# Layer 1's neighbour mix as one 512-column product, in a four-layer graph network on one Trainium2 core

## The chip, the core and the metric

The kernel runs on one core of one Trainium2 chip, in a single launch. The metric is device time in microseconds (us). Before the change three runs gave 3241.18, 3243.03 and 3243.22 us; the median is 3243.03 us. The profiled execution took 3241.16 us, with a span of 3239.2 us from the first to the last instruction and a mean granted TensorE clock of 0.999.

The engines have short names in profiles: PE is TensorE's matmul, PEld its weight load, DVE is VectorE, ACT is ScalarE, POOL is GpSimd, SP is the engine from whose queue nearly all transfers are issued.

## The reference

There are 128 independent batches of 128 nodes with 512 features each, all in float32, and one 128 x 128 adjacency matrix. Four layers follow each other, each with its input added and a layer norm over the features:

```python
x = layernorm(x + einsum('nm,bmd->bnd', adj, x) @ W0 + bias0)          # layer 0
x = layernorm(x + gat(x))                                              # layer 1
x = layernorm(x + maxpool(x))                                          # layer 2
x = layernorm(x + attention(x))                                        # layer 3

def gat(x):                       # W: 512 x 512, a: 1024
    h = x @ W1
    s1, s2 = h @ a[:512], h @ a[512:]
    e = leaky_relu(s1[:, :, None] + s2[:, None, :], 0.2) * adj
    att = softmax(e, axis=2)
    return elu(einsum('bij,bjf->bif', att, h) + beta * h)
```

Layer 2 takes, for every node, the largest value of adj @ x over the features, with a bias and a relu. Layer 3 is attention with 8 heads of 64, masked by adj, with one more layer norm inside it.

The kernel never computes h. In layer 1 it writes (att + beta * I) @ x @ W1: first a mix of the nodes of x, then one product with W1. The logits come from x @ (W1 @ a), two row sums per batch. Layer 0 is the same: a mix with adj, then a product with W0.

## The kernel before

Every batch is a chain of steps written as a Python generator. `use(engine, work, take)` asks a planner for a place in an engine's order and for buffers; the planner keeps estimated durations and fixes the order of all engines' instructions when the program is built. On the chip that order is fixed, and semaphores do the waiting. `LANDED` is the planner's allowance for the landing of turned features.

```python
FIRST, PAIRS = 2, 6            # groups of two batches at the start and at the end, else groups of four
SOON = (0, 4, 0, 4, 10, 0)     # how far the last groups' steps are brought forward
SCALED = 2                     # near the end, last layer norms are applied on ScalarE
BUFS = {"ps": 8, "x": 19, "yT": 4, "z": 2, "e": 2, "et": 1, "eT": 2, "ex": 2, "xT": 2, "v": 7,
        "qkT": 2, "pt": 1, "xt": 2}
LAST, AHEAD = 14, 4            # the last 14 batches get a rank 4 earlier
DIRECT = 12                    # layer 0 of the first 12 batches is mixed in the first way
LANDED = 4.0
```

A product needs the features on the partitions (yT, four blocks of 128). There are two ways to get there. The first gives it at once, with four products of 128 columns, in which x itself is the stationary operand; ScalarE copies the result out of PSUM:

```python
def mixed(xb, nodes, first=False):
    b0, b1 = yield use("PE", 0.9, lambda: ("ps", "yT"), late=0.2)
    p = bank(b0, K, P)
    for k in range(K):
        nc.tensor.matmul(p[:, k, :], xb[:, k * P : (k + 1) * P], nodes, start=True, stop=True)
    yT = buf(b1, K, P)
    # ... (first batch: copied in two halves)
    yield use("ACT", 0.6, urgent=True)
    nc.scalar.copy(yT, p)
    give(b0)
    return yT, b1
```

The second multiplies once, 512 columns wide, with the nodes' weights as the stationary operand. The result has nodes on the partitions, and has to be turned: VectorE transposes it in 32 x 32 blocks, one transfer writes it to DRAM, and four transfers read it back so that the blocks land on their partitions. The features then stand in a permuted order, and the weight's rows are loaded in the same order (`permuted`):

```python
def mixed_rows(xb, nodes):
    b0 = yield use("PE", 0.86, "ps", late=0.2)
    p = bank(b0, D)
    nc.tensor.matmul(p, nodes, xb, start=True, stop=True)
    bt = yield use("DVE", 0.71, "xt", urgent=True)
    xt = buf(bt, Q, P)
    nc.vector.transpose(xt.rearrange("p q f -> p (q f)"), p)
    give(b0)
    scratch = yield from to_squares(xt, bt)          # one transfer, 256 KB
    b1 = yield use("SP", 2.0, "yT", late=LANDED)
    yT = buf(b1, K, P)
    from_squares(yT, scratch)                        # four transfers, 64 KB each
    return yT, b1
```

The part of a batch that the change touches:

```python
    direct = i < DIRECT                                                     # layer 0
    yT, by = yield from mixed(xb, adjT, i == 0) if direct else mixed_rows(xb, adjT)
    # ... product with W0, bias, layer norm
    yield wa_ready                                                          # layer 1
    yield use("DVE", 1.7)
    for j in range(2):
        scr = one.tile([P, D], F32, name="scr")
        nc.vector.scalar_tensor_tensor(scr, xb, 1.0, wa_rows[:, j, :], ..., accum_out=gr.s[:, b, j : j + 1])
    done(gr.logits[h])

    yield gr.attention[h]
    yT, by = yield from mixed(xb, gr.eT[h][:, b % 2])
    gr.read(h, 2)
    bp = yield use("PE", 3.44, "ps", late=0.2)
    p = product(bp, lambda k: yT[:, k, :], lambda k: w1_sb[:, k, :])
    give(by)
    # ... elu, layer norm, layer 2
    # layer 3: x turned as in mixed_rows into xT; queries and keys for a whole group (128, 256 or
    # 512 columns), values, scores, softmax, turned weights, weighted values, projection, two norms
```

In `product` every matmul has 512 columns, and four of them add up over the features. Queries and keys (L621) are computed for a group at once: 512 columns in a group of four, 256 in a group of two. Each matmul of the source appears as two MATMUL instructions in the trace. Line numbers of the profile: L270 is `mixed`, L289 is `mixed_rows`, L292 its transpose, L281 ScalarE's copy in `mixed`, L262 `product`, L670 scores, L691 weighted values, L325 the writes to DRAM, L311 the four reads.

Of the kernel before, what the change touches and what calls it, by code (L numbers as in the profile page):

```python
# [8 lines left out]
F32 = mybir.dt.float32  # L9
# [6 lines left out]
P = 128  # L16
D = 512
K = D // P
G = 4
FIRST, PAIRS = 2, 6  # L20
SOON = (0, 4, 0, 4, 10, 0)
WHOLE = 2
SCALED = 2
H = 8
HD = D // H
S = 32
Q = P // S
# [4 lines left out]

BUFS = {
    "ps": 8,
    "x": 19, "yT": 4, "z": 2, "e": 2, "et": 1, "eT": 2, "ex": 2, "xT": 2, "v": 7, "qkT": 2,
    "pt": 1, "xt": 2,
}
LAST, AHEAD = 14, 4
DIRECT = 12
LATER = 18  # L40
LANDED = 4.0
MARGIN = 1.0
LAND, ROW_LAND = 2.0, 0.0053

# [6 lines left out]
class Plan:  # L51
# [14 lines left out]
    def use(self, engine, work, take=None, late=0.05, urgent=False, follow=False):  # L66

        names = take if callable(take) else lambda: (take,) if take else ()
        return engine, work, names, late, 0 if follow else 1 if urgent else 2
# [67 lines left out]
def gnn_stack_kernel(  # L141
# [17 lines left out]
    nc = tc.nc  # L159
# [3 lines left out]
    const = ctx.enter_context(tc.tile_pool(name="const", bufs=1))  # L163
    work = ctx.enter_context(tc.tile_pool(name="work", bufs=1))
    small = ctx.enter_context(tc.tile_pool(name="small", bufs=12))
    one = ctx.enter_context(tc.tile_pool(name="one", bufs=1))
    ps = ctx.enter_context(tc.tile_pool(name="ps", bufs=1, space=PSUM))

    plan = Plan()
# [2 lines left out]
    def buf(slot, *shape):  # L172
        return work.tile([P, *shape], F32, name="{}_{}".format(*slot))
# [153 lines left out]
    def from_rows(dst, scratch):  # L327

        nc.sync.dma_start(dst, scratch.rearrange("(a r) c f -> (r c) a f", a=Q))
# [47 lines left out]
    def matrix(dst, src):  # L377
        nc.sync.dma_start(dst, src.rearrange("(k p) o -> p k o", p=P))

    def loads():  # L380
        yield use("SP", 0.4)
        nc.sync.dma_start(adj_sb, adj)
        landing(adj_in, P // 4)
        yield from load(0, "ACT", nc.scalar)
        w0_slot.append((yield use("SP", 0.0, "qkT")))
        w0_nat.append(
            buf(w0_slot[0], G, 2 * K, P).rearrange("p b c n -> p (b c n)")[:, : K * D].rearrange(
                "p (k o) -> p k o", k=K
            )
        )  # L390
        for k in range(K):
            yield use("SP", 0.4)
            nc.sync.dma_start(w0_nat[0][:, k, :], w0[k * P : (k + 1) * P])
            landing(w0_chunk[k], P)
        yield from load(1)
        yield use("SP", 0.4)
        nc.sync.dma_start(bias0_sb, rows(bias0, D))
        landing(bias0_in, P)
        for i in range(2, 4):
            yield from load(i)  # L400
        slot = yield use("SP", 1.0, "pt")
        matrix(w1_sb, w1)
        a_sb = buf(slot, H, P).rearrange("p (s k) f -> p s (k f)", s=2)
        nc.sync.dma_start(a_sb, rows(a, 2 * D).rearrange("p (s f) -> p s f", s=2))
        landing(w1_in, (K + 2) * P)
        plan.start(logit_rows(a_sb, slot), 0)
        for i in range(4, 8):
            yield from load(i)
        yield use("SP", 2.0)
        permuted(w0_sb, w0)  # L410
        landing(w0_in, K * P)
        yield use("SP", 1.0)
        nc.sync.dma_start(beta1_sb, rows(beta1, 1))
        nc.sync.dma_start(
            b2_sb, bass.AP(tensor=b2.tensor, offset=b2.offset, ap=[[1, P], [1, 1]])
        )
        landing(scalars_in, 2 * P)
        for i in range(8, 12):
            yield from load(i)
        yield use("SP", 2.5)  # L420
        permuted(wqkv_sb, w_qkv)
        matrix(wproj_sb, w_proj)
        for dst, src in ((bproj_sb, b_proj), (gamma_sb, gamma), (beta3_sb, beta3)):
            nc.sync.dma_start(dst, rows(src, D))
        landing(w3_in, (4 * K + 3) * P)
        for i in range(12, NB):
            yield from load(i)
# [34 lines left out]
    def logit_rows(a_sb, slot):  # L462

        yield w1_in
        wa = const.tile([P, K, 2], F32, name="wa")
        for s in range(2):
            for k in range(K):
                yield use("DVE", 0.8)
                scr = one.tile([P, D], F32, name="scr")
                nc.vector.scalar_tensor_tensor(  # L470
                    scr, w1_sb[:, k, :], 1.0, a_sb[:, s, :], op0=ALU.mult, op1=ALU.mult,
                    accum_out=wa[:, k, s : s + 1],
                )
        give(slot)
        for s in range(2):
            b0 = yield use("PE", 0.5, "ps", late=0.2, urgent=True)
            p = bank(b0, K, P)
            for k in range(K):
                nc.tensor.transpose(p[:, k, :], wa[:, k, s : s + 1].to_broadcast([P, P]), ident)
            yield use("DVE", 0.7, urgent=True)  # L480
            nc.vector.tensor_copy(wa_rows[:, s, :], p.rearrange("p k f -> p (k f)"))
            give(b0)
        done(wa_ready)

# [58 lines left out]
    def attention1(gr, h):  # L543
        yield gr.logits[h]
        yield scalars_in
        s = gr.s

        yield use("DVE", 0.2)
        st = small.tile([P, 2, Q, S // Q], F32, name="s2")
        nc.vector.transpose(  # L550
            st.rearrange("p i c u -> p i u c"),
            s[:, 2 * h : 2 * h + 2, 1:2, None].to_broadcast([P, 2, S // Q, Q]),
        )
        row = dram.tile([2 * Q, Q, S // Q], F32, name="s_d")
        yield use("SP", 0.5, late=2.0)
        nc.sync.dma_start(
            row.rearrange("j a u -> a j u"), st[::S].rearrange("p i c u -> p (i c) u")
        )
        bz = yield use("SP", 0.5, "z", late=2.2)
        z = buf(bz, 2, P)  # L560
        nc.sync.dma_start(
            z, row.rearrange("j a u -> (j a u)")[None, :].to_broadcast([P, 2 * P]).rearrange(
                "p (i f) -> p i f", i=2
            ),
        )
        be = yield use("DVE", 2.1, "e", urgent=True)
        nc.vector.tensor_tensor(
            z, z, s[:, 2 * h : 2 * h + 2, 0:1].to_broadcast([P, 2, P]), op=ALU.add
        )
        e = buf(be, 2, P)  # L570
        nc.vector.scalar_tensor_tensor(e, z, ALPHA, z, op0=ALU.mult, op1=ALU.max)
        give(bz)
        nc.vector.tensor_tensor(
            e, e, adj_cols.rearrange("p c r -> p (c r)")[:, None, :].to_broadcast([P, 2, P]),
            op=ALU.mult,
        )
        nmx = small.tile([P, 2], F32, name="nmx")
        nc.vector.tensor_reduce(nmx, e, axis=AX.X, op=ALU.max, negate=True)
        yield use("ACT", 1.2)
        sums = small.tile([P, 2], F32, name="sums")  # L580
        for i in range(2):
            nc.scalar.activation(
                e[:, i, :], e[:, i, :], AF.Exp, bias=nmx[:, i : i + 1],
                accum_out=sums[:, i : i + 1],
            )
        bt = yield use("DVE", 1.5, "et")
        rs = small.tile([P, 2], F32, name="rs")
        nc.vector.reciprocal(rs, sums)
        et = buf(bt, Q, 2, S)
        for i in range(2):  # L590

            nc.vector.scalar_tensor_tensor(
                e[:, i, :], e[:, i, :], rs[:, i : i + 1], beta_id, op0=ALU.mult, op1=ALU.add
            )
            nc.vector.transpose(et[:, :, i, :], e[:, i, :].rearrange("p (c r) -> p c r", c=Q))
        give(be)
        scratch = dram.tile([P, Q, 2 * S], F32, name="e_d")
        yield use("SP", 0.5, late=2.0)
        to_rows(et.rearrange("p c i s -> p c (i s)"), scratch)
        give(bt)  # L600
        gr.slot[h] = yield use("SP", 0.5, "eT", late=3.8)
        eT = buf(gr.slot[h], Q, 2 * S)
        from_rows(eT, scratch)
        gr.eT[h] = eT.rearrange("p a (i s) -> p i a s", i=2)
        done(gr.attention[h])


# [118 lines left out]
    def batch(i):  # L726
# [22 lines left out]
        give(bp)  # L749
        yield from layernorm_act(xb)  # L750
        yield wa_ready
        yield use("DVE", 1.7)
        for j in range(2):
            scr = one.tile([P, D], F32, name="scr")
            nc.vector.scalar_tensor_tensor(  # L755
                scr, xb, 1.0, wa_rows[:, j, :], op0=ALU.mult, op1=ALU.mult,
                accum_out=gr.s[:, b, j : j + 1],
            )
        done(gr.logits[h])


        yield gr.attention[h]
        yT, by = yield from mixed(xb, gr.eT[h][:, b % 2])
        gr.read(h, 2)
        bp = yield use("PE", 3.44, "ps", late=0.2)
        p = product(bp, lambda k: yT[:, k, :], lambda k: w1_sb[:, k, :])
# [109 lines left out]
    def usual(i, xb, oT, valued, biased):  # L876
# [8 lines left out]
        mv, rstd = yield from mean_rstd(o)  # L885
        yield added
        yield use("DVE", 1.9)
        t1 = one.tile([P, D], F32, name="t1")
        nc.vector.scalar_tensor_tensor(  # L889
            t1, o, mv[:, 0:1], gamma_sb, op0=ALU.subtract, op1=ALU.mult  # L890
        )
# [114 lines left out]
```

## Time and profile before

| | before |
|---|---|
| median time, 3 runs | 3243.03 us |
| span of the profiled execution | 3239.2 us |
| instructions | 40,147 |
| TensorE busy | 3225.9 us, 100% |
| VectorE busy | 2627.0 us, 81% |
| ScalarE busy | 1183.2 us, 37% |
| GpSimd busy | 932.6 us, 29% |
| moved by transfers | 366.15 MB, 732,167 packets |
| share of 16 DMA engines, main queue | 40.1% |
| mix as four products, L270 | 1024 instructions for layer 1, 96 for layer 0 |
| mix as one product, L289 | 232 instructions for layer 0 |

The busy share is an average over the span. The chain of work that ended last is followed back from the last instruction: at each step to what released it, or to the instruction before it on its engine. A group's line gives its line, engine, operation, tiles (output<-inputs), shapes and count, then busy time and the mean of one instruction in ns, and after the second bar the idle time of the engine just before these instructions, with what ended most of it. Matmuls are pipelined: one can start while the one before it still runs, so that the time from start to start is shorter than the duration shown.

### The profile page before, as it was taken

How to read it: one execution, taken by the hardware profiler on the slowest of the kernel's cores; microseconds unless marked ns; L12 is line 12 of the kernel's file. 1: busy time of each engine (PE TensorE's matmuls, PEld its weight loads, DVE VectorE, ACT ScalarE, POOL GpSimd, SP SyncE). 2: the span in 40 equal slices, each digit the busy share in tenths (PEclk: the TensorE clock that was granted, in tenths of full speed). 3: DMA queues.
4: the chain of work that ended last, by engine and by line, in shares of the span. 5: the costliest groups of instructions: out<-in, count | busy, mean ns of one | idle time of the engine just before them, and what ended most of it. 6: DMA issues, size and time to landing. Idle time of an engine off the chain costs nothing.

```text
span 3239.2 us, 40147 instructions
## 1 busy us (share of the span) xinstructions
PE 3225.9 (100%) x12135; PEld 1665.6 (51%) x12135; DVE 2627.0 (81%) x5649; ACT 1183.2 (37%) x3477; POOL 932.6 (29%) x1033
## 2 busy tenths in 40 slices
PE   9999999999999999999999999999999999999998
PEld 5645455545455455554555545555455454455565
DVE  7888777887878878888788787887878877888867
ACT  2444333333342333433334333343233432333432
POOL 3322222232332323323223232232322322323222
PEclk9999999999999999999999999999999999999999
DMA  6234333444334443344433444334443344442432
GB/s 216 78 103 119 105 101 93 135 122 127 86 94 134 123 125 88 100 129 120 127 96 91 127 122 129 108 78 124 123 128 108 91 110 129 127 121 70 125 91 98
DMA packets 732167, 366.15 MB, mean 113 GB/s; under 512 B 566192, under 2 KB 648496, under 8 KB 731952
## 3 DMA queue, kind: packets, MB, share of 16 engines
q1 hardware_dynamic: 731808, 363.33, 40.1%
q8 instruction: 97, 1.59, 0.2%
q14 instruction: 118, 0.97, 0.1%
q10 hardware_dynamic: 144, 0.26, 0.0%
HBM read 190.38 MB, written 173.08 MB: 112 GB/s over the span
## 4 chain that ended last, share of the span: by engine, by line
PE 98%; DVE 1%; DMA 1%; issue 0%; POOL 0%; SPq 0%; ACT 0%; POOLq 0%; DVEq 0%; ACTq 0%
PE ps L262 54%; PE ps L621 26%; PE ps L270 4%; PE ps L670 4%; PE ps L691 4%; PE ps L783 3%; PE ps L289 3%; DMA p_d<-pt 0%; DMA x_d<-xt 0%; DVE st L191 0%; PE ps L921 0%; DVE t L889 0%; DVE pt L843 0%; DMA yT<-x_d 0%; PE ps L434 0%
## 5 line engine op out<-in xcount | busy, mean ns | idle before, releaser
L621 PE MATMUL ps<-xT,wqkv_sb 128*128 128x512 f32 (+1 forms) x2304 | 886.0, 545 | 0.0
L205 POOL TENSOR_TENSOR rstd<-ve,neghalf 128x1 f32<-128x1 f32 x640 | 436.7, 682 | 1482.7 <-DVE ve L199 1226.2
L262 PE MATMUL ps<-w_sb,yT 128*128 128x512 f32 x1952 | 858.9, 593 | 1.6 <-DMA yT<-x_d 1.6
L621 PEld LDWEIGHTS ps<-xT,wqkv_sb 128*128 128x128 f32 x2304 | 438.1, 190 | 445.4 <-issue 417.9
L262 PEld LDWEIGHTS ps<-w_sb,yT 128*128 128x128 f32 x1952 | 370.3, 190 | 463.1 <-issue 444.1
L262 PE MATMUL ps<-wqkv_sb,xT 128*128 128x512 f32 x1024 | 448.3, 593 | 0.0
L262 PE MATMUL ps<-wproj_sb,v 128*128 128x512 f32 x1016 | 445.6, 595 | 0.7 <-ACT v L863 0.7
L833 ACT ACTIVATE qkT<-qkT,nmx 128x128 f32<-128x128 f32 x1008 | 389.1, 389 | 12.6 <-DVE nmx L819 12.6
L191 DVE BATCH_NORM_STATS2 st<-x 128x6 f32<-128x512 f32 x510 | 348.3, 683 | 38.4 <-ACT x L791 36.2
L255 POOL TENSOR_TENSOR x<-x,v 128x512 f32<-128x512 f32 x127 | 171.7, 1352 | 556.3 <-DVE v L882 554.1
L262 PEld LDWEIGHTS ps<-wqkv_sb,xT 128*128 128x128 f32 x1024 | 193.9, 190 | 240.4 <-issue 225.8
L262 PEld LDWEIGHTS ps<-wproj_sb,v 128*128 128x128 f32 x1016 | 191.0, 190 | 233.0 <-issue 227.0
L225 ACT ACTIVATE x<-x,nmr,rstd 128x512 f32<-128x512 f32 x257 | 204.1, 807 | 187.7 <-DVE nmr L223 185.9
L630 ACT ACTIVATE qkT<-ps 128x512 f32<-128x512 f32 (+1 forms) x144 | 77.4, 549 | 428.9 <-PE ps L621 425.8
L255 POOL TENSOR_TENSOR x<-x,beta_sb 128x512 f32<-128x512 f32 x128 | 165.9, 1298 | 233.2 <-DVE xt L798 218.1
L791 ACT ACTIVATE x<-x,mx 128x512 f32<-128x512 f32 x128 | 91.4, 718 | 335.1 <-DVE mx L789 330.4
L843 DVE STREAM_TRANSPOSE pt<-qkT 128x1024 f32<-128x1024 f32 x128 | 158.5, 1238 | 59.8 <-DMA p_d<-pt 59.4
L812 DVE TENSOR_TENSOR qkT<-ps,maskb 128x512 f32<-128x512 f32 x256 | 161.2, 683 | 46.1 <-PE ps L670 42.7
L771 ACT ACTIVATE ex<-ps 128x512 f32<-128x512 f32 x128 | 76.4, 597 | 330.3 <-PE ps L262 330.3
L755 DVE SCALAR_TENSOR_TENSOR scr<-x,wa_rows 128x512 f32<-128x512 f32 x256 | 183.1, 715 | 10.4 <-ACT x L225 5.9
L833 ACT ACTIVATION_READ_ACCUMULATOR qkT<-qkT,nmx 128x1 f32 x1008 | 190.8, 189 | 0.0
L632 ACT COPY qkT<-ps 128x512 f32<-128x512 f32 (+1 forms) x144 | 76.0, 539 | 298.1 <-PE ps L621 298.0
(91 smaller groups left out, 3615.1 us busy)
## 6 DMA issues: line engine op xcount, KB each, us to landing
p_d<-pt SPq DMA_DIRECT2D x128, 512.0 KB
qkT<-p_d SPq DMA_DIRECT2D x128, 512.0 KB
x_d<-xt SPq DMA_DIRECT2D x244, 256.0 KB
xT<-x_d SPq DMA_DIRECT2D x512, 64.0 KB
x<-in_x SPq DMA_DIRECT2D x127, 256.0 KB
out<-x SPq DMA_DIRECT2D x127, 256.0 KB
yT<-x_d SPq DMA_DIRECT2D x464, 64.0 KB
z<-s_d SPq DMA_DIRECT2D x64, 128.0 KB
```

The costliest lines, as they stand in the source:

```text
L191: nc.vector.bn_stats(st, src)
L205: nc.gpsimd.tensor_tensor(rstd, ve, neghalf, op=ALU.pow)
L225: nc.scalar.activation(xb, xb, AF.Identity, bias=nmr, scale=rstd)
L255: nc.gpsimd.tensor_tensor(dst, dst, other, op=ALU.add)
L262: nc.tensor.matmul(p, lhs(k), rhs(k), start=(k == 0), stop=(k == K - 1))
L270: nc.tensor.matmul(p[:, k, :], xb[:, k * P : (k + 1) * P], nodes, start=True, stop=True)
L621: nc.tensor.matmul(p[:, j, :], wqkv_sb[:, k, (c + j) * P : (c + j + 1) * P], gr.xT[:, k, : gr.size * P], start=(k == 0), stop=(k == K - 1),)
L670: nc.tensor.matmul(p[j][:, c, :], gr.qkT[rws, b, c, :], gr.qkT[rws, b, K + c, :], start=True, stop=True,)
L755: nc.vector.scalar_tensor_tensor(scr, xb, 1.0, wa_rows[:, j, :], op0=ALU.mult, op1=ALU.mult, accum_out=gr.s[:, b, j : j + 1],)
L812: nc.vector.tensor_tensor(pr[:, j * K : (j + 1) * K], sc[j], maskb[:, None, :].to_broadcast([P, K, P]), op=ALU.add,)
L833: nc.scalar.activation(pr[:, j, :], pr[:, j, :], AF.Exp, bias=nmx[:, j : j + 1], accum_out=sums[:, j : j + 1],)
L843: nc.vector.transpose(pt.rearrange("p c h s -> p h c s"), pr.rearrange("p h (c r) -> p h c r", c=Q))
```

## The change

Layer 1's mix, too, is done in the second way: one 512-column product, turned by VectorE and by transfers. W1 is loaded with permuted rows, the row vectors for the logits are put back in natural order as they are copied out of PSUM, and the attention weights are loaded by two transfers so that each batch's weights are contiguous and can be a stationary operand. Two scratch tiles are given up: `scr` is taken from the buffers of the exponentials, `t1` is written in place. Their space goes to one more buffer of x (20) and one more of mixed features (5). The order at the end is set anew: four pairs at the end in place of six, other ranks, the last 16 batches brought forward instead of 14, one more layer norm on ScalarE. The planner's allowance for turned features goes from 4.0 to 4.5.

The purpose is to take the four 128-column products and ScalarE's copy out of layer 1.

```diff
-FIRST, PAIRS = 2, 6
-SOON = (0, 4, 0, 4, 10, 0)
+FIRST, PAIRS = 2, 4
+SOON = (0, 0, 0, -4, 10, 0)
-SCALED = 2
+SCALED = 3
-    "x": 19, "yT": 4, ...
+    "x": 20, "yT": 5, ...
-LAST, AHEAD = 14, 4
+LAST, AHEAD = 16, 4
-LANDED = 4.0
+LANDED = 4.5
-    one = ctx.enter_context(tc.tile_pool(name="one", bufs=1))
...
-        slot = yield use("SP", 1.0, "pt")
-        matrix(w1_sb, w1)
+        slot = yield use("SP", 2.5, "pt")
+        permuted(w1_sb, w1)
...
-                yield use("DVE", 0.8)
-                scr = one.tile([P, D], F32, name="scr")
+                b_scr = yield use("DVE", 0.8, "ex")
+                scr = buf(b_scr, D)
+                give(b_scr)
...
-            nc.vector.tensor_copy(wa_rows[:, s, :], p.rearrange("p k f -> p (k f)"))
+            nc.vector.tensor_copy(
+                wa_rows[:, s, :].rearrange("p (q k r) -> p k r q", q=Q, k=K),
+                p.rearrange("p k (r q) -> p k r q", q=Q),
+            )
...
-        gr.slot[h] = yield use("SP", 0.5, "eT", late=3.8)
-        eT = buf(gr.slot[h], Q, 2 * S)
-        from_rows(eT, scratch)
-        gr.eT[h] = eT.rearrange("p a (i s) -> p i a s", i=2)
+        gr.slot[h] = yield use("SP", 1.0, "eT", late=3.8)
+        eT = buf(gr.slot[h], 2, Q, S)
+        for i in range(2):
+            from_rows(eT[:, i], scratch[:, :, i * S : (i + 1) * S])
+        gr.eT[h] = eT.rearrange("p i a s -> p i (a s)")
...
-        yield use("DVE", 1.7)
+        b_scr = yield use("DVE", 1.7, "ex")
         for j in range(2):
-            scr = one.tile([P, D], F32, name="scr")
+            scr = buf(b_scr, D)
...
-        yT, by = yield from mixed(xb, gr.eT[h][:, b % 2])
+        yT, by = yield from mixed_rows(xb, gr.eT[h][:, b % 2])
...
-        t1 = one.tile([P, D], F32, name="t1")
+        t1 = o
```

More of the change, by code (lines that the diff above doesn't have):

```diff
@@ L34 @@
     "ps": 8,
-    "x": 19, "yT": 4, "z": 2, "e": 2, "et": 1, "eT": 2, "ex": 2, "xT": 2, "v": 7, "qkT": 2,
+    "x": 20, "yT": 5, "z": 2, "e": 2, "et": 1, "eT": 2, "ex": 2, "xT": 2, "v": 7, "qkT": 2,
     "pt": 1, "xt": 2,
 }
-LAST, AHEAD = 14, 4
+LAST, AHEAD = 16, 4
 DIRECT = 12
 LATER = 18
-LANDED = 4.0
+LANDED = 4.5
 MARGIN = 1.0
@@ L758, in batch @@
             )
+        give(b_scr)
         done(gr.logits[h])
         yield gr.attention[h]
-        yT, by = yield from mixed(xb, gr.eT[h][:, b % 2])
+        yT, by = yield from mixed_rows(xb, gr.eT[h][:, b % 2])
         gr.read(h, 2)
```

## The prediction

> **What bounds the kernel now.** I read four views in this order: the shares of the span, the chain of work that ended last, the groups of instructions, and then stretches of the TensorE and queue timelines. First the page:
>
> ```profile
> PE 3225.9 (100%) x12135; PEld 1665.6 (51%) x12135; DVE 2627.0 (81%) x5649; ACT 1183.2 (37%) x3477; POOL 932.6 (29%) x1033
> PE 98%; DVE 1%; DMA 1%; issue 0%; POOL 0%; SPq 0%; ACT 0%; POOLq 0%; DVEq 0%; ACTq 0%
> L262 PE MATMUL ps<-w_sb,yT 128*128 128x512 f32 x1952 | 858.9, 593 | 1.6 <-DMA yT<-x_d 1.6
> ```
>
> TensorE is busy for the whole span, and 98% of the chain that ended last is TensorE work. Busy time alone would not settle it, because matmuls overlap (a mean of 593 ns is listed for instructions that follow each other more closely than that). The last column of the third line does: the largest group waited 1.6 us in all, once, for a transfer of turned features. Nearly every microsecond is one TensorE instruction behind another, so only two things can change the time: fewer TensorE nanoseconds, or a hole that is not there today.
>
> The two ways of mixing stand side by side in the chain in order of time (start, length, engine, tile, line, count):
>
> ```profile
> 61.83 1.78 PE ps L270 x16
> 63.61 1.72 PE ps L289 x4
> 65.33 17.17 PE ps L262 x40
> ...
> 2952.69 3.77 PE ps L670 x64
> 2956.46 3.64 PE ps L691 x64
> 2960.11 13.93 PE ps L262 x32
> 2974.04 13.81 PE ps L621 x64
> ```
>
> L270 is the mix as four 128-column products, 8 instructions a batch, so 16 are two batches: 0.89 us each. L289 is the mix as one 512-column product, 2 instructions a batch, so 4 are two batches: 0.86 us each. Layer 1 uses the first form today, layer 0 the second from batch 12 on.
>
> **What the Trainium skill says.** "TensorE: Matmul & The Clock Gate", section Back-to-back issue gap, gives 518 cycles for 512 columns and 134 for 128: one long instruction saves 3.4% against four short ones (518 against 536). "FP8 and Floating Point Precision", section TensorE Precision Notes, says that true FP32 takes four passes. Together, as an estimate at 2.4 GHz: 4 x 518 cycles are 0.863 us, 4 x 4 x 134 cycles are 0.893 us. The trace has 0.86 and 0.89, so both pages agree with it. "Perfetto Trace Analysis", section Identifying the Most-Contended Engine, warns that matmul occupancy is a poor measure of headroom; the 593 ns above bear that out, so I count start to start. "DMA: Bandwidth & Descriptors", section Latency and other measured facts, speaks of a fixed cost of about 2 us for a transfer; a write of turned features here takes about 2.7 us before its readers are issued (below), which agrees.
>
> **The change part by part.**
>
> *TensorE, mix.* 128 batches x (0.89 - 0.86) us = 3.8 us less. All of it is on the path, since TensorE is the path. The product after it (8 instructions, 3.43 us) does not change; permuting the rows of the weight alters only its load.
>
> *TensorE, end order.* Two pairs of batches become one group of four. The last stretch of the chain has a pair's queries and keys at 13.81 us (x64, 256 columns), and elsewhere a group of four's at 27.47 us (x64, 512 columns): 27.62 against 27.47. A pair's scores and weighted values take 1.99 and 1.90 us (x32), 7.78 us for two pairs; four batches take 3.77 + 3.64 = 7.41 us as shown. A stream of products that follows the small ones costs 0.2 us extra (13.93 instead of 13.73 us), once instead of twice. Sum: 0.15 + 0.37 + 0.2, about 0.7 us less.
>
> *TensorE, the one stall.* The planner's allowance for turned features goes from 4.0 to 4.5 us. The 1.6 us hole was a landing later than 4.0 allowed, so I count 1.0 of it as gone.
>
> *VectorE.* It gains 128 transposes of 128x512 out of PSUM; the same instruction takes 706 ns median on layer 0's mix. That is 90 us: 2627 becomes about 2717 us, 84% of the span. ScalarE loses 128 copies of 586 ns, 75 us. Neither is on the path by its sum. The two scratch tiles now come from buffers shared with the exponentials; t1 is written in place. Those cost no instruction.
>
> *Transfers.* Each batch adds one write and four reads of 64 KB. A batch's four reads take 2.54 us of the queue, so 128 x 2.54 = 325 us of issue time; the writes add about 0.33 us each, 42 us, and the second load of eT 64 x 0.37 = 24 us. Together 12% of the span more on a queue that today spends 610 us waiting for finished rows to store. On the DMA engines, packets go from 732,000 to about 1.03 million (a 64 KB read lands in runs of 32 floats, 128 bytes, so it is 512 packets; 128 x 4 x 512 = 262,000, and some 40,000 for the writes and the split load of eT). With the mean packet of today (40.1% of 16 engines over 731,808 packets is 28 ns) that would be at most 15 points more, 55% busy. No bound is reached.
>
> *Latency.* This is what can cost something. These are lines of the queue's timeline (start, length, engine, line, transfer, count):
>
> ```profile
> 61.69 2.15 SPq L325 DMA_DIRECT2D x_d<-xt  x2
> 65.49 5.32 SPq L311 DMA_DIRECT2D yT<-x_d  x8
> ...
> 1499.86 0.32 SPq L325 DMA_DIRECT2D x_d<-xt  x1
> 1502.58 2.57 SPq L311 DMA_DIRECT2D yT<-x_d  x4
> ```
>
> In the middle the write goes out at 1499.86 and its readers at 1502.58, 2.7 us later; they take 2.6 us to issue, and I put their landing at another 2.2 us. With the transpose, 0.7 + 2.7 + 2.6 + 2.2 = 8.2 us stand where a ScalarE copy of 0.59 us stood: each batch stays in work some 7.6 us longer. A batch needs 3239 / 128 = 25.3 us of TensorE, so 7.6 us are 0.3 batches more in flight; one more x buffer and one more yT buffer more than pay for that. In the steady part I expect no new hole, since TensorE always has other batches' products.
>
> At the start it is different. At 61.83 us the first two batches of layer 1 are mixed, just after the first layer-0 batches of the turned kind; at 65.33 two layer-1 products begin at once and bridge the wait for those layer-0 features, whose reads go out only at 65.49 to 70.8. After the change both kinds wait. The first features can be there at about 65.5 + 2.6 + 2.2 = 70 us, so a hole of up to 5 us opens at 65.3. Up to three mixes of later, already loaded batches (0.86 us each) can fill part. I count **2 us** (from 0 to 5), and TensorE never gets it back, for it has no slack later.
>
> **Sum.** 3243.0 - 3.8 - 0.7 - 1.0 + 2.0 = **3239.5 us**.
>
> **The rivals.** (a) *The wait replaces the copy.* Features arrive late again and again because the queue issues in order and a store of finished rows can block the reads behind it. For it: the queue's largest wait is 610 us for finished rows, with single waits up to 19 us. Against it: layer 0 already works like this in 116 batches and TensorE lost 1.6 us. If one layer-1 read in ten were 1 us late, it would cost 13 us: about 3252 us. (b) *VectorE becomes the bound in stretches.* It was already 89.6 us busy in 100 to 200 us. With the transposes it would pass 93 there, and its order is fixed. Against it: scores and exponentials wait in PSUM banks, and all eight are shared in turn, so short bursts are absorbed. If it bites, 3 to 10 us, in the first 200 us. (c) *The end drains worse.* The last batches' path is longer by 7.6 us. Against it: the last layer-1 mix stands at 3099 us, 140 us ahead of the end, and the last 16 instead of 14 batches are now brought forward. If it fails, 3 to 8 us in the last 140 us. (d) *Everything is hidden, the start too*: 3237.5 us.
>
> **Range and chances.** The three gains are at most 3.8 + 0.7 + 1.6 = 6.1 us; with 1 us between executions (3241.2 to 3243.2 before) and a count of the mix rounded to 0.01 us the low end is 3234.5. The high end takes a 5 us hole at the start and some of rivals (a) to (c) on top: 3250. Two per cent are 65 us: no gain of that size is there to be had, and a loss of it needs half a microsecond a batch of repeated waits. Within 2%: 0.97; slower by over 2%: 0.02; faster by over 2%: 0.01. That the time falls at all I hold for about two in three.
>
> **What would show it.** L270 should keep only the 96 instructions of the direct batches, and the one-product mix should appear x256 more, at 0.86 us a batch. In the chain, TensorE should stay at 98%. VectorE should read about 2717 us, ScalarE about 1108. A hole should stand between 60 and 75 us with "DMA yT<-x_d" as releaser; its length tells my 2 us right or wrong. The steady part should show no wait of TensorE; the period of four batches, 100.45 us now (the chain's 27.47 us pieces of L621 begin at 1467.24 and 1567.69), should become about 100.3. I am wrong if waits on yT recur through the middle, if TensorE waits for a PSUM bank that VectorE holds, or if the last 140 us grow.

## The result and the profile after

The change made the kernel slower: 3402.09 us (median of 5 runs, 3400.03 to 3405.22) against 3241.25 us in the same comparison, a ratio of 1.0496 (95% interval 1.0482 to 1.0510). That is 161 us more, far outside the range of 3234.5 to 3250. In the listing of the changed kernel the first lines stand one earlier than before: L269 is `mixed`, L288 `mixed_rows`, L291 its transpose, L261 `product`, L324 the writes, L310 the four reads, L224 the layer norm on ScalarE. L788 is layer 2's product, L625 queries and keys.

The page of the changed kernel, its shares of the span and its chain by engine; below them, the packets of the main queue:

```profile
PE 3269.1 (96%) x11303; PEld 1586.4 (47%) x11303; DVE 2744.4 (81%) x5777; ACT 1116.0 (33%) x3342; POOL 947.0 (28%) x1033
q1 hardware_dynamic: 1054416, 430.48, 48.1%
DVE 39%; PE 31%; DMA 16%; SPq 8%; issue 4%; POOL 1%; ACT 1%; DVEq 0%; POOLq 0%; ACTq 0%
```

Read the third line first. TensorE carried 98% of the chain before; now it carries 31%, and VectorE, transfers and the issuing queue (SPq) carry 63%. No share of busy time tells this: VectorE still reads 81% and the DMA engines 48%. TensorE's idle time is the span less its busy time, 3400.2 - 3269.1 = 131 us, against 13 us before. The other 43 us are inside its busy time. A 512-column matmul that is followed at once counts 429 ns from start to start, one that nothing follows counts its whole 592 ns, and the mean granted clock fell from 0.999 to 0.995; how the 43 us divide between the two was not taken apart.

What TensorE waited for (line, releaser, total, times, longest):

```profile
PE ps L788 <- ACT x L224: 55.4, 47, 2.8
PE ps L261 <- DMA yT<-x_d: 21.0, 21, 2.6
PE ps L695 <- DVE qkT L817: 9.3, 19, 1.2
PE ps L261 <- DVE x L229: 8.8, 13, 1.2
PE ps L261 <- DMA e_d<-et: 5.3, 1, 5.3
```

Only 21 us are waits for turned features. The largest part is layer 2's product (L788), which waits for the layer norm of layer 1 on ScalarE. That norm waited for VectorE: 521.7 of the 566.1 us that ScalarE stood idle before it ended with VectorE's nmr. The page's line for it, and then what VectorE waited for:

```profile
L224 ACT ACTIVATE x<-x,nmr,rstd 128x512 f32<-128x512 f32 x258 | 207.5, 809 | 566.1 <-DVE nmr L222 521.7
```
```profile
DVE z L570 <- DMA z<-s_d: 149.2, 56, 9.3
DVE pt L848 <- DMA p_d<-pt: 100.8, 31, 4.9
DVE xt L291 <- DMA x_d<-xt: 95.5, 44, 7.1
DVE xt L803 <- DMA x_d<-xt: 49.7, 29, 3.9
```

VectorE stood 395 us for these transfers. In the kernel before it was 132 us:

```profile
DVE z L567 <- DMA z<-s_d: 65.1, 46, 4.2
DVE pt L843 <- DMA p_d<-pt: 59.4, 44, 3.5
DVE xt L292 <- DMA x_d<-xt: 7.2, 4, 3.1
```

Here z holds the broadcast logits of a later pair of batches, xt is a tile of turned features and pt one of turned attention weights of layer 3, both still being written out. VectorE works in its fixed order, so while it waits for one of them, the layer norms behind it wait too.

One such stretch, in the chain in order of time, shows the knot (start, length, what):

```profile
1854.88 2.28 DMA x_d<-xt
...
1859.10 0.63 SPq L310
...
1861.80 0.63 SPq L310
...
1862.47 3.18 DMA z<-s_d
1865.67 0.44 DVE z L570
```

The queue issues eight reads of turned features, two batches of layer 1, from 1857.18 to 1862.42. The load of z (128 KB) stands behind them in the same queue, goes out at 1862.47, and VectorE stands still for it (2.79 us in the timeline of VectorE) until 1865.67.

The order of every engine comes from the kernel's own planner, so its durations can be held against the trace. It gives a batch's four reads 2.0 us of the queue. In the trace they take 4 x 0.63 us with gaps between, about 2.7 us from the first start to the next issue. It lets a write land after 0.5 + 2.3 = 2.8 us; where the queue stood waiting for a write, the trace has 2.5 us at the median from the write's issue to the first read, and 3.4 us at the upper quarter. So the reads are planned too short throughout, the writes only in their slow part. By the planner's sums, which come out of the kernel when it is built, VectorE is taken for 3024 us of 3232 and the queue for 1356 us, where the kernel before had 2934 and 1003 us of 3234. The plan promised 3232 us, and the chip ended 170 us later; the kernel before ended 7 us after its plan.

### The profile page after: what moved, and what is told of

Read it like the earlier page. It is cut to its first block, busy times and chain, and to the rows that moved or that the text cites. A ratio compares the mean times of both kernels' runs of the same rounds, so it can differ in the third digit from the quotient of the medians.

```text
span 3400.2 us, 39331 instructions
## 1 busy us (share of the span) xinstructions
PE 3269.1 (96%) x11303; PEld 1586.4 (47%) x11303; DVE 2744.4 (81%) x5777; ACT 1116.0 (33%) x3342; POOL 947.0 (28%) x1033
## 3 DMA queue, kind: packets, MB, share of 16 engines
q1 hardware_dynamic: 1054416, 430.48, 48.1%
## 4 chain that ended last, share of the span: by engine, by line
DVE 39%; PE 31%; DMA 16%; SPq 8%; issue 4%; POOL 1%; ACT 1%; DVEq 0%; POOLq 0%; ACTq 0%
PE ps L261 17%; PE ps L625 9%; SPq L310 7%; DMA x_d<-xt 7%; DVE st L190 6%; DMA z<-s_d 5%; DMA p_d<-pt 3%; DVE pt L848 3%; DVE x L229 3%; DVE ex L759 3%; DVE qkT L845 2%; DVE v L894 2%; DVE xt L291 2%; DVE qkT L817 2%; DVE mv L196 2%
## 5 line engine op out<-in xcount | busy, mean ns | idle before, releaser
L261 PE MATMUL ps<-w_sb,yT 128*128 128x512 f32 x1952 | 871.0, 597 | 39.7 <-DMA yT<-x_d 21.0
L625 PE MATMUL ps<-xT,wqkv_sb 128*128 128x512 f32 (+1 forms) x2240 | 886.4, 556 | 0.0
L625 PEld LDWEIGHTS ps<-xT,wqkv_sb 128*128 128x128 f32 x2240 | 425.5, 190 | 456.9 <-issue 428.8
L261 PEld LDWEIGHTS ps<-w_sb,yT 128*128 128x128 f32 x1952 | 368.2, 191 | 523.6 <-issue 441.2
L261 PE MATMUL ps<-wqkv_sb,xT 128*128 128x512 f32 x1024 | 456.2, 593 | 0.0
L261 PE MATMUL ps<-wproj_sb,v 128*128 128x512 f32 x1016 | 444.8, 595 | 0.7 <-ACT v L868 0.7
L224 ACT ACTIVATE x<-x,nmr,rstd 128x512 f32<-128x512 f32 x258 | 207.5, 809 | 566.1 <-DVE nmr L222 521.7
L261 PEld LDWEIGHTS ps<-wqkv_sb,xT 128*128 128x128 f32 x1024 | 194.8, 191 | 244.2 <-issue 226.3
L261 PEld LDWEIGHTS ps<-wproj_sb,v 128*128 128x128 f32 x1016 | 190.7, 190 | 235.2 <-issue 229.3
L291 DVE STREAM_TRANSPOSE xt<-ps 128x512 f32<-128x512 f32 x244 | 167.3, 704 | 102.3 <-DMA x_d<-xt 95.5
L848 DVE STREAM_TRANSPOSE pt<-qkT 128x1024 f32<-128x1024 f32 x128 | 157.8, 1233 | 101.1 <-DMA p_d<-pt 100.8
L759 DVE SCALAR_TENSOR_TENSOR ex<-x,wa_rows 128x512 f32<-128x512 f32 x256 | 200.2, 782 | 26.9 <-ACT x L224 22.4
L229 DVE TENSOR_SCALAR x<-x,mv,rstd 128x512 f32<-128x512 f32 x252 | 179.1, 711 | 15.8 <-POOL rstd L204 15.3
L788 PE MATMUL ps<-x,adjT 128*128 128x512 f32 x256 | 137.4, 625 | 56.3 <-ACT x L224 55.4
L254 POOL TENSOR_TENSOR x<-x,bias_sb 128x512 f32<-128x512 f32 x128 | 184.4, 1444 | 23.7 <-PE ps L269 11.1
```

The source lines that it names most:

```text
L224: nc.scalar.activation(xb, xb, AF.Identity, bias=nmr, scale=rstd)
L229: nc.vector.tensor_scalar(xb, xb, mv[:, 0:1], rstd, op0=ALU.subtract, op1=ALU.mult)
L254: nc.gpsimd.tensor_tensor(dst, dst, other, op=ALU.add)
L261: nc.tensor.matmul(p, lhs(k), rhs(k), start=(k == 0), stop=(k == K - 1))
L625: nc.tensor.matmul(p[:, j, :], wqkv_sb[:, k, (c + j) * P : (c + j + 1) * P], gr.xT[:, k, : gr.size * P], start=(k == 0), stop=(k == K - 1),)
L848: nc.vector.transpose(pt.rearrange("p c h s -> p h c s"), pr.rearrange("p h (c r) -> p h c r", c=Q))
```

## The experiments

I set out with two theories. **Q**: the queue falls behind a plan that is too cheap for it, and VectorE waits for the queue. **V**: VectorE itself has too much work with 128 transposes more. Two smaller rivals: **S**, the shared scratch tiles, and **E**, the end order.

### The mix put back, and the mix alone

```diff
 # mix_taken_back: the changed kernel with
-        yT, by = yield from mixed_rows(xb, gr.eT[h][:, b % 2])
+        yT, by = yield from mixed(xb, gr.eT[h][:, b % 2])
 # (and the natural loads of W1, wa_rows and eT);  mix_alone: the kernel before with the opposite edit
```

> The changed kernel with layer 1's mix put back to four products and ScalarE's copy; the shared scratch, t1 in place, 20 x and 5 yT buffers, the end order and the allowance of 4.5 stay. Theory Q (the transfer queue: the added reads take 2.5 us a batch where the planner gives them 2.0, the queue falls behind the planned order, VectorE, which works in a fixed order, then waits for z and for buffers being written out, and has too little slack to catch up): 3240 to 3255 us, since nothing of the added traffic is left. Theory V (VectorE alone has too little slack, 128 transposes more): the same. Theory S (the scratch tiles that became shared buffers, or t1 in place, make VectorE wait or slower): 3300 us or more stays. Theory E (the end order): the last 250 us keep most of a loss.

> The kernel before with layer 1's mix alone done as one product, turned by VectorE and transfers (with the loads that this needs); scratch tiles, 19 x, 4 yT, end order and allowance of 4.0 as before. Theory Q and theory V: the loss is all here, 3380 to 3460 us, a little more than with the whole change because buffers are fewer. Theory S and theory E: under 3290 us.

Measured: 3252.54 us with the mix taken back (ratio 1.0032, 1.0020 to 1.0044), 3414.54 us with the mix alone (1.0534, 1.0516 to 1.0551). The loss is in the mix; S is out. Not all of mix_alone's 173 us is lateness on the chip: its own plan ends at 3281 us, 47 us after that of the kernel before. The rest of the change (buffers, order, allowance) taken together helps the mix by about 12 us (3414.5 against 3402.1). On the four-product mix the same rest costs 11 us, and these stand at the end. The plan of mix_taken_back already has a hole of 6.8 us at 3215 us; the trace has one of 5.2 us at 3220, and a granted clock of 0.64 from 3225 to 3236:

```profile
PE ps L691 <- DMA qkT<-p_d: 5.2, 1, 5.2
```

Whether the end order alone or its meeting with other buffers makes this hole, no run separates.

### Half of the logit sums

```diff
-                scr, xb, 1.0, wa_rows[:, j, :], op0=ALU.mult, op1=ALU.mult,
+                scr[:, : D // 2], xb[:, : D // 2], 1.0, wa_rows[:, j, : D // 2], op0=ALU.mult, op1=ALU.mult,
```

> The changed kernel with the two logit sums of layer 1 taken over half of the columns only (the other half is left out); every engine's order is untouched. VectorE gets some 0.55 us a batch back, 70 us in all. Theory V: the loss is VectorE's own load, so more than half of the 160 us goes: 3300 us or less. Theory Q: VectorE waits for the queue just as before and uses the saved time only to catch up between; 20 to 60 us less, 3340 to 3380 us.

Measured: 3383.25 us. Half of each sum was left out; VectorE's busy time fell by 65 us, from 2744.4 to 2679.0, and the time by 19 us. Its waits did not shrink: 163.9 us for z, 111.3 us for xt (L291). This speaks against V, which asked for 3300 us or less. It lies just outside Q's range of 3340 to 3380.

### The same bytes in fewer or larger reads

In these three kernels layer 1's features are read back unsorted, so the sorting is left out; the planner's numbers and every order stay as in the changed kernel.

```diff
-        from_squares(yT, scratch)                                  # 4 x 512 packets of 128 bytes
+        # plain_reads: one of 256 KB, whole rows
+        nc.sync.dma_start(yT.rearrange("p k f -> p (k f)"), scratch.rearrange("p q f -> p (q f)"))
+        # or four_large_reads
+        for k in range(K):
+            nc.sync.dma_start(yT[:, k, :], scratch[:, k, :])
+        # or two_small_reads
+        src = scratch.rearrange("p q (m h s) -> p h (q m) s", h=2, s=S)
+        for h in range(2):
+            nc.sync.dma_start(yT[:, 2 * h : 2 * h + 2].rearrange("p k (m s) -> p (k m) s", s=S), src[:, h])
```

> The changed kernel with the four reads of layer 1's turned features made one read of the same 256 KB in whole rows (their features stay unsorted, that sorting is left out); orders and the planner's numbers untouched. It takes some 2.2 us of the queue's time a batch away and 260,000 small packets, nothing of VectorE's work. Theory Q: most of the loss goes, 3240 to 3280 us. Theory V: the loss stays, 3370 us or more.

> As the run with one plain read, but as four reads of 64 KB in runs of 512 bytes (sorting left out): the count of issues of the changed kernel with a quarter of its packets. If the number of issues is what makes the queue late: 3370 us or more. If it is the packets of 128 bytes (in issue time or in landing): near the one plain read, 3255 to 3290 us.

> As the run with one plain read, but as two reads of 128 KB in runs of 128 bytes (another wrong order; sorting left out): half of the issues of the changed kernel with all of its 2048 packets. If a read's time on the queue goes with its packets, the two take as long as the four, 2.5 us, and the loss stays: 3360 to 3410 us. If it goes with the issues, they take half: 3270 to 3320 us.

| layer 1's reads | packets a batch | queue a batch | time |
|---|---|---|---|
| four, runs of 128 bytes (the change) | 2048 | 4 x 0.63 = 2.5 us | 3402.1 us |
| four, runs of 512 bytes | 512 | 4 x 0.43 = 1.7 us | 3307.2 us |
| two, runs of 128 bytes | 2048 | 2 x 0.66 = 1.3 us | 3307.2 us |
| one, whole rows | 128 | 0.32 us | 3258.8 us |

The times of one read come from the transfers' own rows (count, then shortest, median and longest in ns), one line from each of the three kernels:

```profile
L298 SPq DMA_DIRECT2D yT<-x_d x512: 314/430/1678, 74.7 to 3105.9; - x171
```
```profile
L299 SPq DMA_DIRECT2D yT<-x_d x256: 517/658/2058, 75.2 to 3104.9; - x128
```
```profile
L297 SPq DMA_DIRECT2D yT<-x_d x128: 314/320/662, 74.8 to 3054.2; - x128
```

One plain read fell in Q's range. Four large reads ended between the two answers that I had set out: it is not the number of issues alone, since they give back 95 us. Two small reads ended as the second answer said, at half the time on the queue: it is not the packets alone, since with all 2048 of them they give back 95 us too. (The two equal times are two measurements, with spans of 3305.2 and 3305.4 us.) The time on the queue goes roughly along with the result, although 1.7 and 1.3 us end at the same place. Both are below the 2.0 us that the plan allows, and still 66 us are lost; so a read's queue time above its price is not the whole of the loss. With one plain read VectorE does all its transposes, is busier than in any other run, and waits far less for z and for xt (its page, then its waits):

```profile
PE 3230.5 (99%) x11303; PEld 1591.1 (49%) x11303; DVE 2776.0 (85%) x5777; ACT 1118.7 (34%) x3342; POOL 947.3 (29%) x1033
```
```profile
DVE pt L853 <- DMA p_d<-pt: 98.3, 33, 5.1
DVE z L575 <- DMA z<-s_d: 52.8, 33, 6.6
DVE xt L291 <- DMA x_d<-xt: 13.8, 12, 3.9
```

The wait for pt is as long as in the changed kernel (98.3 us against 100.8) with only 18 us of loss left, so the loss does not hang on it. VectorE busy for 85% with TensorE at 99% rules V out: the same work on VectorE is no obstacle once the queue keeps up.

### The planner's prices corrected, nothing else

```diff
-        b1 = yield use("SP", 2.0, "yT", late=LANDED)          # and the same in layer 3's features
+        b1 = yield use("SP", 2.7, "yT", late=LANDED)
-        yield use("SP", 0.5, late=2.3)                        # the write
+        yield use("SP", 0.5, late=3.2)
```

> The changed kernel with the planner's numbers for the transfer queue alone set to what the traces show: 2.7 in place of 2.0 us for the four reads (both in layers 0 and 1 and before layer 3), 3.2 in place of 2.3 us for the landing of a write. No operation changes; orders on all engines are planned anew. The planner's own end moves from 3232 to 3265 us. Theory Q in the form that the plan was too cheap for the queue: the chip comes within 30 us of the plan, 3265 to 3295 us. If the queue is simply overloaded whatever the order, or VectorE is the bound: 3360 us or more.

Measured: 3265.48 us (1.0072, 1.0055 to 1.0089), where its plan promised 3264.8. Not one operation differs from the changed kernel; 137 of the 161 us are gone by ordering them with higher prices. The price of the reads is now that of the trace. That of a write is not: 0.5 + 3.2 = 3.7 us lies above even the upper quarter of 3.4, so it is room for slow writes and not a truer middle. What is left stands in the plan itself, which has a hole of 21.2 us at 2822 us; the chip has it at the same place, 15.1 us long (TensorE's waits in queue_priced):

```profile
PE ps L625 <- DMA xT<-x_d: 15.1, 1, 15.1
PE ps L788 <- ACT x L224: 4.2, 2, 3.0
```

L788's wait is 4.2 us, from 55.4. Which of the two prices was it?

> The changed kernel with one planner's number corrected, the four reads at 2.7 instead of 2.0 us (landing of a write stays at 2.3); plan 3275.4 us. If the queue's own time is the mis-sized term, the chip keeps the plan within 25 us: 3275 to 3300 us. If it is the landing of the writes: 3330 us or more.

> The changed kernel with the other number alone corrected, the landing of a write at 3.2 instead of 2.3 us (reads stay at 2.0); plan 3268.9 us. If the queue's own time is the mis-sized term, the queue still falls behind the plan and the chip is 50 us or more above it: 3320 to 3380 us. If it is the landing, 3270 to 3290 us.

Measured: 3308.2 us with the reads alone corrected (33 us over its plan of 3275.4), 3321.1 us with the landing alone (52 us over 3268.9). Both ended between the two answers that I had set out. The first takes 94 of the 161 us away, the second 81, and only both together make the chip keep its plan, which the changed kernel missed by 170 us. So the mis-sized term is the turning path of the plan: 0.7 us on the queue, and too little room for slow writes. The reads' part looks somewhat larger; each of the two was measured once, and each has another order.

### A plan with true prices, searched for its shortest end

With the prices near the traces (2.7 for the reads, 0.65 and 2.7 or 3.3 for a write, 1.2 for eT, 0.55 for z) I searched order, ranks, allowance, margin, the number of direct batches and the split of the 27 tiles over x, yT and xt for the shortest plan. The best version on the chip:

```diff
-SOON = (0, 0, 0, -4, 10, 0)
+SOON = (-4, 10, 4, 10, 10, 0)
-    "x": 20, "yT": 5, ... "xt": 2
+    "x": 20, "yT": 3, ... "xt": 4
-LAST, AHEAD = 16, 4      DIRECT = 12      LANDED = 4.5      MARGIN = 1.0
+LAST, AHEAD = 14, 4      DIRECT = 14      LANDED = 3.0      MARGIN = 0.5
 # and the prices above
```

> Layer 1's mix as one product, with the planner's queue numbers near what the traces show (2.7 us for four reads, 0.65 and 3.3 for a write, 1.2 for eT) and end order, ranks and the split of 27 tiles over x (21), mixed features (3) and turned ones (3) chosen again for the shortest plan, 3229.4 us. Theory Q: the chip keeps such a plan, as it kept 3265, so 3231 to 3241 us, faster than both kernels; the four-product mix is then at a disadvantage of some 4 us. If instead the chip can't keep a plan with VectorE so full: 3260 us or more.

> The same with the landing of a write planned at 2.7 in place of 3.3 and an allowance of 4.0 for turned features, 22 x, 3 and 2 tiles; plan 3229.0 us. The traces have landings of 2.5 us at the median but 3.5 at the upper quarter, so theory Q expects some waits of VectorE for writes: 3233 to 3260 us, not better than the safer plan.

> The same prices, but four tiles for turned features (20 x, 3 mixed) and an allowance of 3.0; plan 3228.8 us. With four tiles VectorE should not wait for a write to leave (5 us or less in all, against 145 in the changed kernel). Theory Q: 3232 to 3255 us; if the allowance of 3.0 is too short, TensorE waits on yT.

> Layer 1's mix as four products with ScalarE's copy, everything else (prices, search for order and tiles) as in the replanned runs: plan 3232.8 us. It tells what the better order gives without the one-product mix. 3234 to 3245 us; against the best one-product plan 3 to 5 us slower, the mix's share.

| | plan | chip | ratio to before (95% interval) |
|---|---|---|---|
| replanned_safe | 3229.4 us | 3238.76 us | 0.9993 (0.9985 to 1.0001) |
| replanned | 3229.0 us | 3237.86 us | 0.9990 (0.9983 to 0.9997) |
| replanned_xt4 | 3228.8 us | 3237.58 us | 0.9988 (0.9981 to 0.9994) |
| replanned_four (four products) | 3232.8 us | 3239.37 us | 0.9994 (0.9986 to 1.0002) |

The version with four tiles for turned features beats both kernels: 4.8% faster than the changed one, 0.12% faster than the one before, with an interval that stays below 1. Its page, and then the longest of VectorE's waits for transfers:

```profile
PE 3220.3 (100%) x11315; PEld 1586.3 (49%) x11315; DVE 2707.9 (84%) x5775; ACT 1122.0 (35%) x3344; POOL 933.7 (29%) x1033
PE 97%; DMA 1%; DVE 1%; SPq 0%; issue 0%; ACT 0%; POOL 0%; POOLq 0%; DVEq 0%; ACTq 0%
```
```profile
DVE pt L848 <- DMA p_d<-pt: 40.7, 29, 4.4
DVE z L570 <- DMA z<-s_d: 40.6, 26, 9.3
DVE xt L291 <- DMA x_d<-xt: 4.4, 7, 1.0
```

TensorE is the chain again, at 97%, and VectorE's wait for tiles being written out is 4.4 us, as expected (5 or less). The safer prices did not pay: the plan with a landing of 2.7 was no worse than the one with 3.3, against what I had expected. How much of the 3.7 us is the one-product mix and how much the better order isn't settled: against replanned_four the gain is 1.8 us where I expected 3 to 5, and the intervals overlap.

## Why the prediction was wrong

**The bound before** was read rightly: TensorE, 98% of the chain, no slack.

**The mix's saving** of 3.8 us has the right size where nothing else is in the way: TensorE's busy time is 3224.8 us in replanned_four and 3220.3 us in replanned_xt4 (which mixes two batches more in the first way). L269 kept the 96 instructions of the direct batches in the changed kernel and L288 gained 256, as foreseen.

**The step that failed** is the one on transfers with its verdict "No bound is reached", and with it "In the steady part I expect no new hole". I added 391 us of issue time to the queue and judged it by its share. What happened in its place is that the added reads held back other transfers in the same queue: VectorE's waits for transfers went from 132 to 395 us, and TensorE, behind VectorE's layer norms, stood idle for 131 us instead of 13. The steady period of four batches, forecast at 100.3 us, became 105.9 to 107.6 us. The numbers that mattered stood in the same text and in the same code: four reads take 2.54 us in the trace, and the planner has 2.0. The kernel before has that error in 116 + 128 batches as well; the change adds 128 more. Why it cost nothing there stays open. The planned slack of VectorE, 300 us before and 208 after, is one candidate, but it was not tried alone, and half_logits speaks against it: 65 us less work gave back only 19. The DMA engines themselves stayed far from full: by the prediction's own numbers the added packets are about 16 points and not "at most 15", and 48.1% was measured against 40.1%.

**Rival (a)** named the mechanism, a late queue, and mis-sized it twelvefold: 13 us against 161. I counted lateness only where TensorE meets yT directly. That part measured 21.0 us; the rest came by way of z, of tiles being written out, and of layer norms behind them on VectorE. The sign that I had named, waits on yT through the middle, was there: 21 of them. **Rival (b)**, VectorE as the bound, fell with the plain read; between 100 and 200 us VectorE was busy for 86.1 us, not the 93 that it would have taken. **Rival (c)**: the end cost nothing that shows. TensorE idled for 10 us in the last 400 us of the changed kernel, and for 11 us in the last 140 us of the kernel before.

**The hole at the start** was foreseen and too small. I expected 2 us between 60 and 75 us. These are the rows of TensorE's timeline (start, length, instruction, and in brackets the idle time before):

```profile
68.63 1.13 PE L288 MATMUL ps<-x,eT 128*128 128x512 f32 x2 [1.52 <-DVE xt L291]
75.94 8.23 PE L261 MATMUL ps<-w_sb,yT 128*128 128x512 f32 x14 [5.33 <-DMA e_d<-et]
```

That is 1.52 + 5.33 us, and the stretch after it runs on a lower clock (below). The releaser that I had named, DMA yT<-x_d, is not in these rows. The view gives a write of attention weights (e_d<-et), which this product does not read; what it reads are turned features, whose eight reads were issued from 66.99 to 72.60 us. That they ended the wait is likely, and not shown. replanned_xt4 mixes 14 batches directly and has 0.93 us of waiting on yT there.

**The end order** was to bring 0.7 us. It brought none that could be seen, and in place of the one stall of 1.6 us there are 21 waits of 21.0 us in all.

## What to carry to other kernels

When a program fixes each engine's order in advance, compare every duration its plan uses with the trace before judging a change, and its slow part too, not only its middle. With the same two prices too short, one kernel ended 7 us after its plan and the next 170 us. A queue's share of busy time doesn't show this; look at what stands behind its longest issues in the same queue, and at which engine waits for that. And when a change that should be free loses 5%, correct the plan before giving up the change: here nearly the same operations in another order were 0.12% faster than the kernel before.

## What was not expected of the hardware

The queue's time for one transfer depends on its form, at the median: 0.32 us for 128 packets of 2 KB, 0.43 us for 128 of 512 bytes, 0.63 us for 512 of 128 bytes, and 0.66 us for 1024 of 128 bytes. Twice the packets in one issue cost almost nothing more, so fewer and longer issues are cheaper than many of 64 KB.

After the hole of 5.33 us TensorE's granted clock was 0.51 from 76 to 80 us; there the 512-column instructions were 0.85 us apart instead of 0.43. The view of windows shows it in the column after the engines (PEclk):

```profile
76.00:80.00 4.00, 4.00 (x5) 1.79 (x6) 3.86 (x12) 0.81 (x1) 0.80 (x1) 0.51 0.53 84
80.00:90.00 10.00, 10.00 (x24) 4.37 (x23) 5.79 (x15) 1.39 (x5) 0.13 (x1) 1.00 0.66 141
```

So a long hole costs more than its length, here about 1.7 us for four instructions. "TensorE: Matmul & The Clock Gate" in the Trainium skill, section Part 1, describes such a drop to half speed after idle time; the 0.51 agrees.
